# Row statistics moved from VectorE to ScalarE, and a column spread by TensorE instead of two small DMAs, in a four-layer graph network

## The chip, the cores and the metric

The kernel runs on one core of a Trainium2 chip. A core has five engines that run their own instruction streams and meet through semaphores: TensorE (PE, matrix products; the profile lists its weight loads apart as PEld), VectorE (DVE), ScalarE (ACT), GpSimd (POOL), and SyncE (SP), which here only issues DMAs. Products land in PSUM; everything else lives in SBUF. The metric is the device time of one execution in microseconds; lower is better.

## The reference, cut to what matters

There are 128 batches of 128 nodes with 512 features, in float32, and one weighted adjacency matrix of 128x128. Four layers follow each other, each with a residual and a normalisation of every row of 512:

```python
def _layernorm(x):                      # mean and variance over the 512 features of a row
    m, v = mean(x), var(x)
    return (x - m) / sqrt(v + 1e-5)

x = _layernorm(x + (adj @ x) @ W0 + bias0)                       # layer 0
h = x @ W1; s1 = h @ a[:512]; s2 = h @ a[512:]                   # layer 1
e = leaky_relu(s1[:, None] + s2[None, :]) * adj
x = _layernorm(x + elu(softmax(e) @ h + beta * h))
x = _layernorm(x + max over features of relu(adj @ x + b))       # layer 2, per node
q, k, v = split(x @ Wqkv)                                        # layer 3, 8 heads of 64
o = softmax(mask(q @ k.T / 8)) @ v @ Wproj + bproj
x = _layernorm(x + o + _layernorm(o) * gamma + beta3)
```

Layer 1 adds a row logit s1, one number per node, and a column logit s2, which is computed as one number per partition as well but is needed along the free dimension of every partition. Layer 2's term is one number per node. There are five normalisations per batch, 640 in all: one after each layer and one of o.

## The kernel before, in words

A batch is one SBUF tile x of 128 partitions (nodes) by 512 features; 16 such tiles are in flight. `batch(i)` is a Python generator with the chain of steps of one batch through all four layers. Batches are grouped in pairs (G = 2): the pair's queries and keys are computed together (`query_key`, products of 256 columns, L453), and so is layer 1's attention (`attention1`).

The order of the instructions on every engine is fixed at build time by the class `Plan`. Each step asks for an engine with an assumed duration, for buffers, and for a lateness (`yield use("DVE", 0.69, urgent=True)`); `Plan.run` takes again and again the request that can start first, urgent ones and low ranks first among equals, and writes its instructions out in that order. Requests for TensorE are given 1 us after their inputs (MARGIN). So a changed duration or a new step reorders all engines' streams, and on the chip each engine works its stream off strictly in order. The last six batches have ranks lowered by 12, before and after the change alike.

The steps that the change touches:

- `mean_rstd` (L157 to L169): VectorE takes the statistics of a row (`bn_stats`, L161; `bn_aggr`, L163) and adds EPS (L165); GpSimd raises to the power -0.5 (L168). `layernorm_act` then forms -mean*rstd on VectorE (L175) and normalises on ScalarE (L177); `layernorm_dve` normalises on VectorE (L182).
- The operations that write the tile to be normalised: L520 (layer 0: product out of PSUM plus x, VectorE), L545 and L546 (layer 1, VectorE), L561 (layer 2, ScalarE), L647 (o: product plus bias, VectorE), L656 and L659 (layer 3's end, VectorE).
- `attention1` (L376 to L438): the two logits of a pair of batches stand in s, one number per partition; they come from L527, a multiplication with an accumulated sum. The column logits are spread so: VectorE transposes within blocks of 32 (L383), a DMA writes the 256 numbers to memory (L389), a DMA reads them back to every partition (L394, tile z), and VectorE adds the row logit (L400). Leaky relu, adjacency, row maximum, exponential and a transpose through memory (e_d, eT) follow.

Other lines that matter. TensorE: L203 (`mixed`: transposing product into a "tr" bank), L195 (`product`: four accumulating products of 512 columns into an "mm" bank), L554 (layer 2), L583 (scores), L630 (attention times values). PSUM is emptied by ScalarE at L206 (yT), L461 (qkT), L479 (v), L543 (ex), L639 (oT) and by VectorE at L463, L520, L557, L590, L647. Layer 3's probabilities are normalised at L607 and L608, turned at L611 (pt), written by a DMA (p_d) and read back turned (prT) for L630. GpSimd also does three additions per batch (L188). At the start, L342 spreads the columns of W1*a over the partitions with eight TensorE transposes of a broadcast column.

```python
yield use("DVE", 1.0)
nc.vector.bn_stats(st, src); nc.vector.bn_aggr(mv, st)
...
nc.gpsimd.tensor_tensor(rstd, ve, neghalf, op=ALU.pow)
```

Of the kernel before, what the change touches and what calls it, by code (L numbers as in the profile page):

```python
# [8 lines left out]
F32 = mybir.dt.float32  # L9
AF = mybir.ActivationFunctionType  # L10
ALU = mybir.AluOpType
# [4 lines left out]
P = 128  # L16
D = 512
# [4 lines left out]
S = 32  # L22
Q = P // S
ALPHA = 0.2
EPS = 1e-5
# [2 lines left out]

BUFS = {
    "tr": 3, "mm": 3, "sc": 1,  # L30
    "x": 16, "yT": 3, "z": 2, "e": 2, "et": 1, "eT": 2, "ex": 2, "xT": 2, "v": 8, "qkT": 3,
    "pr": 2, "pt": 1, "xt": 2, "prT": 2, "oT": 2, "o": 2,
}
MARGIN = 1.0
# [8 lines left out]
class Plan:  # L43
# [30 lines left out]
    def give(self, slot):  # L74
        name, i = slot
        self.slots[name][i] = self.now
# [38 lines left out]
def gnn_stack_kernel(  # L115
# [28 lines left out]
    use, give, done = plan.use, plan.give, plan.done  # L144

    def buf(shape, name):
        return work.tile(shape, F32, name=name, bufs=BUFS[name])

    def bank(shape, name):
        return ps.tile(shape, F32, name=name, bufs=BUFS[name])  # L150
# [3 lines left out]
        return bass.AP(tensor=src.tensor, offset=src.offset, ap=[[0, P], [1, n]])  # L154


    def mean_rstd(src):  # L157

        yield use("DVE", 1.0)
        st = small.tile([P, 6], F32, name="st")  # L160
        nc.vector.bn_stats(st, src)  # L161
        mv = small.tile([P, 2], F32, name="mv")
        nc.vector.bn_aggr(mv, st)  # L163
        ve = small.tile([P, 1], F32, name="ve")
        nc.vector.tensor_scalar(ve, mv[:, 1:2], EPS, None, op0=ALU.add)  # L165
# [3 lines left out]
        return mv, rstd  # L169

    def layernorm_act(xb):
        mv, rstd = yield from mean_rstd(xb)
        yield use("DVE", 0.21)
        nmr = small.tile([P, 1], F32, name="nmr")
        nc.vector.tensor_scalar(nmr, mv[:, 0:1], rstd, -1.0, op0=ALU.mult, op1=ALU.mult)  # L175
        yield use("ACT", 0.81)
        nc.scalar.activation(xb, xb, AF.Identity, bias=nmr, scale=rstd)  # L177

    def layernorm_dve(xb):
        mv, rstd = yield from mean_rstd(xb)  # L180
        yield use("DVE", 0.67)
        nc.vector.tensor_scalar(xb, xb, mv[:, 0:1], rstd, op0=ALU.subtract, op1=ALU.mult)  # L182

    def pool_add(dst, other, event, after=None):
        if after:
# [24 lines left out]
    def to_rows(turned, scratch):  # L210

        nc.sync.dma_start(scratch, turned)
# [6 lines left out]
    ident = const.tile([P, P], F32, name="ident")  # L219
# [18 lines left out]
    bproj_sb = const.tile([P, D], F32, name="bproj_sb")  # L238
    gamma_sb = const.tile([P, D], F32, name="gamma_sb")
# [136 lines left out]
    def attention1(gr, h):  # L376
        yield gr.logits[h]
        yield scalars_in
        s = gr.s

        yield use("DVE", 0.2)
        st = small.tile([P, 2, Q, S // Q], F32, name="s2")
        nc.vector.transpose(  # L383
            st.rearrange("p i c u -> p i u c"),
            s[:, 2 * h : 2 * h + 2, 1:2, None].to_broadcast([P, 2, S // Q, Q]),
        )
        row = dram.tile([2 * Q, Q, S // Q], F32, name="s_d")
        yield use("SP", 0.1, late=2.0)
        nc.sync.dma_start(  # L389
            row.rearrange("j a u -> a j u"), st[::S].rearrange("p i c u -> p (i c) u")  # L390
        )
        bz = yield use("SP", 0.1, "z", late=2.2)
        z = buf([P, 2, P], "z")
        nc.sync.dma_start(  # L394
            z, row.rearrange("j a u -> (j a u)")[None, :].to_broadcast([P, 2 * P]).rearrange(
                "p (i f) -> p i f", i=2
            ),
        )
        be = yield use("DVE", 2.1, "e", urgent=True)
        nc.vector.tensor_tensor(  # L400
            z, z, s[:, 2 * h : 2 * h + 2, 0:1].to_broadcast([P, 2, P]), op=ALU.add
        )
        e = buf([P, 2, P], "e")
        nc.vector.scalar_tensor_tensor(e, z, ALPHA, z, op0=ALU.mult, op1=ALU.max)
        give(bz)
# [97 lines left out]
    def batch(i):  # L503
        g, b = divmod(i, G)
        h = b // 2
        yield loaded[i]
        gr, xb = group(g), xs[i]
# [3 lines left out]
        yT, by = yield from mixed(xb, adjT)  # L511
# [4 lines left out]
        p = product(lambda k: yT[:, k, :], lambda k: w0_sb[:, k, :])  # L516
        give(by)
        yield biased
        yield use("DVE", 0.69, urgent=True)
        nc.vector.tensor_tensor(xb, p, xb, op=ALU.add)  # L520
        give(bp)
        yield from layernorm_act(xb)
        yield wa_ready
        yield use("DVE", 1.6)
        for j in range(2):
# [3 lines left out]
                accum_out=gr.s[:, b, j : j + 1],  # L529
# [14 lines left out]
        yield use("DVE", 1.5, urgent=True)  # L544
        nc.vector.scalar_tensor_tensor(xb, p, 0.0, xb, op0=ALU.max, op1=ALU.add)  # L545
        nc.vector.scalar_tensor_tensor(xb, ex, 1.0, xb, op0=ALU.min, op1=ALU.add)  # L546
        give(bp)
        give(be)
        yield from layernorm_act(xb)


        bp = yield use("PE", 0.95, "mm", late=0.2, urgent=True)
        p = bank([P, D], "mm")
        nc.tensor.matmul(p, adjT, xb, start=True, stop=True)  # L554
        yield use("DVE", 0.89, urgent=True)
        mx = small.tile([P, 1], F32, name="mx")
        nc.vector.tensor_reduce(mx, p, axis=AX.X, op=ALU.max)  # L557
        nc.vector.tensor_scalar(mx, mx, b2_sb, 0.0, op0=ALU.add, op1=ALU.max)
        give(bp)
        yield use("ACT", 0.81)  # L560
        nc.scalar.activation(xb, xb, AF.Identity, bias=mx)  # L561
        yield from layernorm_dve(xb)


        bt = yield use("DVE", 0.65, "xt")
# [33 lines left out]
        for j in range(H):  # L599
# [3 lines left out]
                accum_out=sums[:, j : j + 1],  # L603
# [41 lines left out]
        bo = yield use("DVE", 0.69, "o", urgent=True)  # L645
# [6 lines left out]
        mv, rstd = yield from mean_rstd(o)  # L652
        yield added
        yield use("DVE", 1.65)
        t1 = one.tile([P, D], F32, name="t1")
        nc.vector.scalar_tensor_tensor(  # L656
            t1, o, mv[:, 0:1], gamma_sb, op0=ALU.subtract, op1=ALU.mult
        )
        nc.vector.scalar_tensor_tensor(xb, t1, rstd, xb, op0=ALU.mult, op1=ALU.add)  # L659
        give(bo)  # L660
        yield from layernorm_dve(xb)
        yield use("SP", 0.1, late=3.0)
        nc.sync.dma_start(out[i], xb)
        give(x_slot[i])
# [37 lines left out]
```

## Time and profile before

| what | value |
|---|---|
| median of 4 runs | 3357.4 us (3354.33 to 3361.61) |
| the profiled execution, its own time | 3357.86 us |
| its span, first to last instruction | 3355.9 us |
| mean granted TensorE clock | 0.996 |
| VectorE busy | 2663.3 us, 79% |
| ScalarE busy | 1186.7 us, 35% |
| GpSimd busy | 934.5 us, 28% |
| mean DMA rate | 91 GB/s |

The statistics on VectorE: L161 takes 348.1 us for 512 tiles x and 87.4 us for 128 tiles o (680 ns each), L163 116.3 us (182 ns each), L165 98.3 us (154 ns each). On ScalarE, an activation over 512 columns takes 722 ns with a per-partition bias (L561), and 813 ns with bias and scale (L177); reading its accumulated sum is an instruction of its own of 189 ns (L601). On VectorE, reading an accumulated sum takes 81 ns (L527).

In the profile an engine's busy time is the union of its instructions' spans. A group is named by line, engine, operation, and tiles as "written<-read". "Idle before" is the engine's idle time ahead of a group, and the arrow names what ended it. The chain that ended last is followed back from the last instruction, at each step to what released it. Lines of the same kind of work carry different numbers before and after the change, since the change adds five lines to the file.

### The profile page before, as it was taken

The numbers are of one execution on the slowest core, as the hardware profiler recorded it, in microseconds if no ns is written. First come the engines' busy times: TensorE is split into PE (matmuls) and PEld (weight loads), VectorE is DVE, ScalarE is ACT, GpSimd is POOL, SyncE is SP. The second block draws the span as 40 slices with busy tenths as digits, with TensorE's granted clock in tenths as the row PEclk, the third lists the DMA queues.
The fourth block names the chain that finished last, engine by engine and source line by source line (L and its number), as shares of the span: only waits on it lengthen the run. The fifth ranks groups of instructions, "written<-read, shape, count | busy, mean of one in ns | idle before, by whom it ended". The sixth has DMA issues, their size and how long they took to land.

```text
span 3355.9 us, 43540 instructions
## 1 busy us (share of the span) xinstructions
PE 3313.4 (99%) x14601; PEld 2056.5 (61%) x14601; DVE 2663.3 (79%) x5527; ACT 1186.7 (35%) x3457; POOL 934.5 (28%) x1031
## 2 busy tenths in 40 slices
PE   9999999999999999999999999999999999999997
PEld 5666656565656566565665666566665665566565
DVE  7877778868877877878788788788788788878875
ACT  2424333333423333333333333333333333343322
POOL 3221322313232232323133223223122234222221
PEclk9999999999999999999999999999999999999998
DMA  4332322332333232232323223323323322322231
GB/s 162 93 112 77 96 91 65 103 95 86 84 95 89 71 96 101 71 108 78 96 85 101 82 79 88 99 77 93 104 81 97 95 79 82 97 78 91 73 108 69
DMA packets 469711, 304.46 MB, mean 91 GB/s; under 512 B 319216, under 2 KB 401264, under 8 KB 469488
## 3 DMA queue, kind: packets, MB, share of 16 engines
q1 hardware_dynamic: 469488, 301.69, 30.1%
q8 instruction: 116, 1.90, 0.2%
q14 instruction: 107, 0.88, 0.1%
HBM read 158.93 MB, written 142.67 MB: 90 GB/s over the span
## 4 chain that ended last, share of the span: by engine, by line
PE 83%; DVE 11%; DMA 4%; issue 1%; ACT 0%; SPq 0%; POOL 0%; POOLq 0%; DVEq 0%; ACTq 0%
PE mm L195 43%; PE mm L453 25%; PE tr L203 5%; PE sc L583 4%; PE tr L630 4%; PE mm L554 3%; DVE st L161 2%; DVE scr L527 2%; DMA z<-s_d 1%; DMA s_d<-s 1%; DVE x L659 1%; DVE x L182 1%; DVE x L520 1%; DVE mv L163 1%; DVE t L656 0%
## 5 line engine op out<-in xcount | busy, mean ns | idle before, releaser
L195 PE MATMUL mm<-w_sb,yT 128*128 128x512 f32 x2048 | 912.3, 594 | 5.5 <-ACT yT L206 4.5
L453 PE MATMUL mm<-xT,wqkv_sb 128*128 128x256 f32 x4096 | 912.6, 381 | 0.7 <-DVE x L520 0.7
L453 PEld LDWEIGHTS mm<-xT,wqkv_sb 128*128 128x128 f32 x4096 | 772.8, 190 | 140.4 <-issue 27.3
L168 POOL TENSOR_TENSOR rstd<-ve,neghalf 128x1 f32<-128x1 f32 x640 | 413.9, 647 | 1290.1 <-DVE ve L165 1098.1
L195 PEld LDWEIGHTS mm<-w_sb,yT 128*128 128x128 f32 x2048 | 381.2, 190 | 454.4 <-issue 434.5
L195 PE MATMUL mm<-wqkv_sb,xT 128*128 128x512 f32 x1024 | 466.3, 598 | 0.0
L601 ACT ACTIVATE pr<-pr,nmx 128x128 f32<-128x128 f32 x1024 | 398.0, 391 | 190.1 <-DVE nmx L597 189.3
L195 PE MATMUL mm<-wproj_sb,oT 128*128 128x512 f32 x1024 | 463.1, 599 | 1.5 <-ACT oT L639 1.5
L188 POOL TENSOR_TENSOR x<-x,o 128x512 f32<-128x512 f32 x128 | 175.7, 1372 | 896.4 <-DVE o L647 797.9
L161 DVE BATCH_NORM_STATS2 st<-x 128x6 f32<-128x512 f32 x512 | 348.1, 680 | 6.7 <-ACT x L561 5.3
L177 ACT ACTIVATE x<-x,nmr,rstd 128x512 f32<-128x512 f32 x256 | 204.7, 810 | 388.0 <-DVE nmr L175 372.9
L195 PEld LDWEIGHTS mm<-wproj_sb,oT 128*128 128x128 f32 x1024 | 191.9, 191 | 224.7 <-issue 218.7
L195 PEld LDWEIGHTS mm<-wqkv_sb,xT 128*128 128x128 f32 x1024 | 189.6, 190 | 201.2 <-issue 192.0
L590 DVE TENSOR_TENSOR pr<-sc,maskb 128x1024 f32<-128x1024 f32 x128 | 156.0, 1219 | 168.5 <-PE sc L583 168.2
L206 ACT COPY yT<-tr 128x512 f32<-128x512 f32 x256 | 147.3, 582 | 202.4 <-PE tr L203 202.2
L527 DVE SCALAR_TENSOR_TENSOR scr<-x,wa_rows 128x512 f32<-128x512 f32 x256 | 200.4, 783 | 23.1 <-ACT x L177 17.0
L188 POOL TENSOR_TENSOR x<-x,beta_sb 128x512 f32<-128x512 f32 x128 | 171.5, 1342 | 161.2 <-DVE xt L567 147.8
L188 POOL TENSOR_TENSOR x<-x,bias_sb 128x512 f32<-128x512 f32 x128 | 181.6, 1429 | 69.7 <-PE tr L203 61.6
L479 ACT COPY v<-mm 128x512 f32<-128x512 f32 x128 | 74.6, 583 | 337.2 <-PE mm L195 337.1
L601 ACT ACTIVATION_READ_ACCUMULATOR pr<-pr,nmx 128x1 f32 x1024 | 193.1, 189 | 0.0
L182 DVE TENSOR_SCALAR x<-x,mv,rstd 128x512 f32<-128x512 f32 x256 | 161.3, 635 | 15.4 <-POOL rstd L168 14.6
L583 PEld LDWEIGHTS sc<-qkT 64*128 64x128 f32 x2048 | 124.8, 187 | 78.0 <-issue 60.1
(62 smaller groups left out, 3483.8 us busy)
## 6 DMA issues: line engine op xcount, KB each, us to landing
p_d<-pt SPq DMA_DIRECT2D x128, 512.0 KB
prT<-p_d SPq DMA_DIRECT2D x128, 512.0 KB
x<-in_x SPq DMA_DIRECT2D x128, 256.0 KB
x_d<-xt SPq DMA_DIRECT2D x128, 256.0 KB
xT<-x_d SPq DMA_DIRECT2D x512, 64.0 KB
out<-x SPq DMA_DIRECT2D x128, 256.0 KB
z<-s_d SPq DMA_DIRECT2D x64, 128.0 KB
e_d<-et SPq DMA_DIRECT2D x64, 128.0 KB
```

What stands on the lines that cost most here:

```text
L161: nc.vector.bn_stats(st, src)
L168: nc.gpsimd.tensor_tensor(rstd, ve, neghalf, op=ALU.pow)
L177: nc.scalar.activation(xb, xb, AF.Identity, bias=nmr, scale=rstd)
L182: nc.vector.tensor_scalar(xb, xb, mv[:, 0:1], rstd, op0=ALU.subtract, op1=ALU.mult)
L188: nc.gpsimd.tensor_tensor(dst, dst, other, op=ALU.add)
L195: nc.tensor.matmul(p, lhs(k), rhs(k), start=(k == 0), stop=(k == K - 1))
L203: nc.tensor.matmul(p[:, k, :], xb[:, k * P : (k + 1) * P], nodes, start=True, stop=True)
L453: nc.tensor.matmul(p[:, j, :], wqkv_sb[:, k, (c + j) * P : (c + j + 1) * P], gr.xT[:, k, :], start=(k == 0), stop=(k == K - 1),)
L527: nc.vector.scalar_tensor_tensor(scr, xb, 1.0, wa_rows[:, j, :], op0=ALU.mult, op1=ALU.mult, accum_out=gr.s[:, b, j : j + 1],)
L583: nc.tensor.matmul(sc[:, j, c, :], gr.qkT[rws, c, nodes], gr.qkT[rws, K + c, nodes], start=True, stop=True,)
L590: nc.vector.tensor_tensor(pr, sc.rearrange("p j c m -> p (j c) m"), maskb[:, None, :].to_broadcast([P, H, P]), op=ALU.add,)
L601: nc.scalar.activation(pr[:, j, :], pr[:, j, :], AF.Exp, bias=nmx[:, j : j + 1], accum_out=sums[:, j : j + 1],)
```

## The change

`mean_rstd` gets the row's sum from its caller: every operation that writes a tile to be normalised now also accumulates the sum over the row (`accum_out`); additions written as `tensor_tensor` become `scalar_tensor_tensor` with a factor of 1.0 for that. VectorE forms nm, the negative mean; ScalarE squares the tile with nm as bias into a tile that nobody reads, and accumulates the sum of squares; VectorE scales and adds EPS; GpSimd's power is as before. The column logits are spread by two TensorE transposes of a broadcast column into a "tr" bank, and VectorE adds the row logit while reading the bank; the DMAs and the block transpose go. The planner's assumed durations are changed with the steps.

```diff
-    def mean_rstd(src):
-
-        yield use("DVE", 1.0)
-        st = small.tile([P, 6], F32, name="st")
-        nc.vector.bn_stats(st, src)
-        mv = small.tile([P, 2], F32, name="mv")
-        nc.vector.bn_aggr(mv, st)
+    def mean_rstd(src, total):
+
+        yield use("DVE", 0.15)
+        nm = small.tile([P, 1], F32, name="nm")
+        nc.vector.tensor_scalar(nm, total, -1.0 / D, None, op0=ALU.mult)
+        yield use("ACT", 1.0)
+        square = one.tile([P, D], F32, name="square")
+        var = small.tile([P, 1], F32, name="var")
+        nc.scalar.activation(square, src, AF.Square, bias=nm, accum_out=var)
+        yield use("DVE", 0.15)
         ve = small.tile([P, 1], F32, name="ve")
-        nc.vector.tensor_scalar(ve, mv[:, 1:2], EPS, None, op0=ALU.add)
+        nc.vector.tensor_scalar(ve, var, 1.0 / D, EPS, op0=ALU.mult, op1=ALU.add)
         yield use("POOL", 0.65, late=0.1, urgent=True)
...
-        nc.vector.tensor_scalar(nmr, mv[:, 0:1], rstd, -1.0, op0=ALU.mult, op1=ALU.mult)
+        nc.vector.tensor_tensor(nmr, nm, rstd, op=ALU.mult)
...
-        nc.vector.tensor_scalar(xb, xb, mv[:, 0:1], rstd, op0=ALU.subtract, op1=ALU.mult)
+        nc.vector.tensor_scalar(xb, xb, nm, rstd, op0=ALU.add, op1=ALU.mult)
...
-        yield use("DVE", 0.2)
-        st = small.tile([P, 2, Q, S // Q], F32, name="s2")
-        nc.vector.transpose(
-            st.rearrange("p i c u -> p i u c"),
-            s[:, 2 * h : 2 * h + 2, 1:2, None].to_broadcast([P, 2, S // Q, Q]),
-        )
-        row = dram.tile([2 * Q, Q, S // Q], F32, name="s_d")
-        yield use("SP", 0.1, late=2.0)
-        nc.sync.dma_start(
-            row.rearrange("j a u -> a j u"), st[::S].rearrange("p i c u -> p (i c) u")
-        )
-        bz = yield use("SP", 0.1, "z", late=2.2)
-        z = buf([P, 2, P], "z")
-        nc.sync.dma_start(
...
+        b0 = yield use("PE", 0.3, "tr", late=0.2, urgent=True)
+        p = bank([P, 2, P], "tr")
+        for i in range(2):
+            nc.tensor.transpose(p[:, i, :], s[:, 2 * h + i, 1:2].to_broadcast([P, P]), ident)
         be = yield use("DVE", 2.1, "e", urgent=True)
-        nc.vector.tensor_tensor(
-            z, z, s[:, 2 * h : 2 * h + 2, 0:1].to_broadcast([P, 2, P]), op=ALU.add
-        )
+        z = one.tile([P, 2, P], F32, name="z")
+        for i in range(2):
+            nc.vector.tensor_scalar(
+                z[:, i, :].rearrange("p (c r) -> p c r", c=Q),
+                p[:, i, :].rearrange("p (r c) -> p c r", c=Q),
+                s[:, 2 * h + i, 0:1], None, op0=ALU.add,
+            )
+        give(b0)
...
-        yield use("DVE", 0.69, urgent=True)
-        nc.vector.tensor_tensor(xb, p, xb, op=ALU.add)
+        yield use("DVE", 0.78, urgent=True)
+        total = small.tile([P, 1], F32, name="total")
+        nc.vector.scalar_tensor_tensor(
+            xb, p, 1.0, xb, op0=ALU.mult, op1=ALU.add, accum_out=total
+        )
...
+        nc.vector.scalar_tensor_tensor(
+            xb, ex, 1.0, xb, op0=ALU.min, op1=ALU.add, accum_out=total
+        )
...
-        yield use("ACT", 0.81)
-        nc.scalar.activation(xb, xb, AF.Identity, bias=mx)
+        yield use("ACT", 0.92)
+        total = small.tile([P, 1], F32, name="total")
+        nc.scalar.activation(xb, xb, AF.Identity, bias=mx, accum_out=total)
...
-        nc.vector.tensor_tensor(o, p, bproj_sb, op=ALU.add)
+        total = small.tile([P, 1], F32, name="total")
+        nc.vector.scalar_tensor_tensor(
+            o, p, 1.0, bproj_sb, op0=ALU.mult, op1=ALU.add, accum_out=total
+        )
...
+        nc.vector.scalar_tensor_tensor(
+            xb, t1, rstd, xb, op0=ALU.mult, op1=ALU.add, accum_out=total
+        )
```

More of the change, by code (lines that the diff above doesn't have):

```diff
@@ L30 @@
     "tr": 3, "mm": 3, "sc": 1,
-    "x": 16, "yT": 3, "z": 2, "e": 2, "et": 1, "eT": 2, "ex": 2, "xT": 2, "v": 8, "qkT": 3,
+    "x": 16, "yT": 3, "e": 2, "et": 1, "eT": 2, "ex": 2, "xT": 2, "v": 8, "qkT": 3,
     "pr": 2, "pt": 1, "xt": 2, "prT": 2, "oT": 2, "o": 2,
@@ L168, in mean_rstd, with layernorm_act, layernorm_dve @@
         nc.gpsimd.tensor_tensor(rstd, ve, neghalf, op=ALU.pow)
-        return mv, rstd
-    def layernorm_act(xb):
-        mv, rstd = yield from mean_rstd(xb)
+        return nm, rstd
+    def layernorm_act(xb, total):
+        nm, rstd = yield from mean_rstd(xb, total)
         yield use("DVE", 0.21)
         nmr = small.tile([P, 1], F32, name="nmr")
-        nc.vector.tensor_scalar(nmr, mv[:, 0:1], rstd, -1.0, op0=ALU.mult, op1=ALU.mult)
+        nc.vector.tensor_tensor(nmr, nm, rstd, op=ALU.mult)
         yield use("ACT", 0.81)
         nc.scalar.activation(xb, xb, AF.Identity, bias=nmr, scale=rstd)
-    def layernorm_dve(xb):
-        mv, rstd = yield from mean_rstd(xb)
+    def layernorm_dve(xb, total):
+        nm, rstd = yield from mean_rstd(xb, total)
         yield use("DVE", 0.67)
-        nc.vector.tensor_scalar(xb, xb, mv[:, 0:1], rstd, op0=ALU.subtract, op1=ALU.mult)
+        nc.vector.tensor_scalar(xb, xb, nm, rstd, op0=ALU.add, op1=ALU.mult)
     def pool_add(dst, other, event, after=None):
@@ L518, in batch @@
         yield biased
-        yield use("DVE", 0.69, urgent=True)
-        nc.vector.tensor_tensor(xb, p, xb, op=ALU.add)
+        yield use("DVE", 0.78, urgent=True)
[3 more added lines that the diff above has]
+        )
         give(bp)
-        yield from layernorm_act(xb)
+        yield from layernorm_act(xb, total)
         yield wa_ready
@@ L543, in batch @@
         nc.scalar.activation(ex, p, AF.Exp)
-        yield use("DVE", 1.5, urgent=True)
+        yield use("DVE", 1.6, urgent=True)
+        total = small.tile([P, 1], F32, name="total")
         nc.vector.scalar_tensor_tensor(xb, p, 0.0, xb, op0=ALU.max, op1=ALU.add)
-        nc.vector.scalar_tensor_tensor(xb, ex, 1.0, xb, op0=ALU.min, op1=ALU.add)
+        nc.vector.scalar_tensor_tensor(
+            xb, ex, 1.0, xb, op0=ALU.min, op1=ALU.add, accum_out=total
+        )
         give(bp)
         give(be)
-        yield from layernorm_act(xb)
+        yield from layernorm_act(xb, total)
         bp = yield use("PE", 0.95, "mm", late=0.2, urgent=True)
@@ L559, in batch @@
         give(bp)
-        yield use("ACT", 0.81)
-        nc.scalar.activation(xb, xb, AF.Identity, bias=mx)
-        yield from layernorm_dve(xb)
+        yield use("ACT", 0.92)
+        total = small.tile([P, 1], F32, name="total")
+        nc.scalar.activation(xb, xb, AF.Identity, bias=mx, accum_out=total)
+        yield from layernorm_dve(xb, total)
         bt = yield use("DVE", 0.65, "xt")
@@ L644, in batch @@
         give(bo)
-        bo = yield use("DVE", 0.69, "o", urgent=True)
+        bo = yield use("DVE", 0.78, "o", urgent=True)
         o = buf([P, D], "o")
-        nc.vector.tensor_tensor(o, p, bproj_sb, op=ALU.add)
+        total = small.tile([P, 1], F32, name="total")
+        nc.vector.scalar_tensor_tensor(
+            o, p, 1.0, bproj_sb, op0=ALU.mult, op1=ALU.add, accum_out=total
+        )
         give(bp)
@@ L651, in batch @@
         plan.start(pool_add(xb, o, added), i)
-        mv, rstd = yield from mean_rstd(o)
+        nm, rstd = yield from mean_rstd(o, total)
         yield added
-        yield use("DVE", 1.65)
+        yield use("DVE", 1.75)
         t1 = one.tile([P, D], F32, name="t1")
         nc.vector.scalar_tensor_tensor(
-            t1, o, mv[:, 0:1], gamma_sb, op0=ALU.subtract, op1=ALU.mult
+            t1, o, nm, gamma_sb, op0=ALU.add, op1=ALU.mult
         )
-        nc.vector.scalar_tensor_tensor(xb, t1, rstd, xb, op0=ALU.mult, op1=ALU.add)
+        total = small.tile([P, 1], F32, name="total")
+        nc.vector.scalar_tensor_tensor(
+            xb, t1, rstd, xb, op0=ALU.mult, op1=ALU.add, accum_out=total
+        )
         give(bo)
-        yield from layernorm_dve(xb)
+        yield from layernorm_dve(xb, total)
         yield use("SP", 0.1, late=3.0)
```

5 lines of the change are left out of this document (removed).

## The prediction

> **What bounds the kernel now.** I read the busy shares and the slices first, then the chain that ended last, then what TensorE waited for, and last the timeline of the end.
>
> ```profile
> span 3355.9 us, 43540 instructions
> ...
> PE 3313.4 (99%) x14601; PEld 2056.5 (61%) x14601; DVE 2663.3 (79%) x5527; ACT 1186.7 (35%) x3457; POOL 934.5 (28%) x1031
> ...
> PE   9999999999999999999999999999999999999997
> ...
> PE 83%; DVE 11%; DMA 4%; issue 1%; ACT 0%; SPq 0%; POOL 0%; POOLq 0%; DVEq 0%; ACTq 0%
> ```
>
> TensorE is busy in 99% of the span, at 90% or more in 39 of 40 slices; the chain is TensorE for 83%. So an instruction added to TensorE lengthens the kernel by about its own time, and work taken from VectorE (79%) pays only where a TensorE gap goes away. All that can be won is span less busy, 3355.9 - 3313.4 = 42.5 us. What ended those gaps:
>
> ```profile
> PE tr L630 <- DMA prT<-p_d: 8.2, 3, 6.2
> PE mm L195 <- ACT yT L206: 4.5, 3, 2.7
> PE mm L554 <- ACT x L177: 3.9, 4, 2.0
> PE sc L583 <- DVE qkT L463: 3.5, 3, 1.4
> PE tr L203 <- DMA x<-in_x: 2.9, 2, 1.9
> PE tr L308 <- DMA adj_sb<-in_adj: 2.8, 1, 2.8
> PE sc L583 <- DVE pr L590: 1.8, 2, 1.2
> PE mm L195 <- ACT oT L639: 1.5, 2, 0.7
> PE mm L554 <- DVE x L520: 1.3, 1, 1.3
> ```
>
> Columns: who waited for what, us in total, times, the longest. The whole list comes to 33.1 us; 9.1 us after the last matmul make up nearly all of the rest. Gaps ended by VectorE add up to 8.2 (3.5 + 1.8 + 1.3 and smaller ones), by ScalarE to 9.9, by DMAs to 15, of which 6.2 is one gap near the end (first the timeline of TensorE, then three lines of the chain in order of time; start, length, what):
>
> ```profile
> 3327.76 3.70 PE L195 MATMUL mm<-wproj_sb,oT 128*128 128x512 f32 x8 [0.74 <-ACT oT L639]
> 3337.68 1.98 PE L630 MATMUL tr<-prT,v 128*64 128x128 f32 x16 [6.21 <-DMA prT<-p_d]
> 3340.38 6.41 PE L195 MATMUL mm<-wproj_sb,oT 128*128 128x512 f32 x8 [0.73 <-ACT oT L639]
> ...
> 3329.93 1.16 DVE pt L611
> 3331.09 0.02 issue
> 3331.11 2.58 DMA p_d<-pt
> ```
>
> After that gap the same work runs slower: 16 matmuls of L630 in 1.98 us (1.09 at other places), 8 of L195 in 6.41 (3.70 above). The granted clock there is 0.50, and 1.00 after an earlier gap of 2.68 us (at 843).
>
> **The change, part by part.**
>
> *1. Column logits by TensorE.* Removed, per pair of batches: one VectorE transpose (L383), two DMAs (L389, L394) and one addition (L400). Added: two TensorE transposes of 128x128 and two VectorE additions out of PSUM. 64 pairs make 128 transposes. The trace has eight of this form (broadcast column, identity), at L342:
>
> ```profile
> 26.96 0.60 PE L342 MATMUL tr<-ident,wa 128*128 128x128 f32 x4
> 27.39 3.60 PE L195 MATMUL mm<-w_sb,yT 128*128 128x512 f32 x8
> ```
>
> Four take 27.39 - 26.96 = 0.43 us from start to start of what follows, 0.109 each, and the neighbours keep their pace. 128 x 0.109 = **+13.9 us**, all on the path. That an instruction alone lasts 272 ns (its group's mean) is pipeline depth; unpipelined it would be 34.8, my upper end. Lower end: if a pair fell into each of the 24 gaps over 0.15 us that the trace has, 24 x 0.22 = 5.3 would be free, leaving 8.6; the gaps are 1% of the span, so I take 13.9.
>
> The Trainium skill, "TensorE: Matmul & The Clock Gate", Part 4, gives about 275 ns for such a transpose inside a kernel. It agrees with the duration of 272 ns, but taken as the price it would make this term 35.2 us and the whole about 3394; the starts 0.109 apart speak against that.
>
> Each pair of transposes is also a new TensorE wait, for VectorE's logits (L527). What queues behind it is the next product. Nearest row: L554, which also waits for a freshly normalised tile, lost 3.9 + 1.3 = 5.2 us over 128 batches; at that rate 64 pairs lose **+2.6** (bounds 0 and 10: four times the rate). The planner gives PE requests 1 us after their inputs, which is why few such waits show.
>
> SP issues 128 DMAs fewer, and the transfers queued behind them (x_d, p_d, xT) leave earlier. SP had waited 91 us at L389 and 51.7 at L394. Only 3.0 us of mid-kernel TensorE gaps end on a DMA, so 0 is taken, -3 the bound. VectorE had waited 67.2 us for z; it now waits for TensorE instead.
>
> *2. Variance on ScalarE.* VectorE loses 640 of each of L161, L163 and L165: 348.1 + 87.4 + 116.3 + 98.3 = 650.1 us. It gains 1280 one-column operations (nm, ve) at L165's 154 ns, 197.1, and 512 accumulator reads at 81 ns (from L527's), 41.5. Part 1 there: -17.7 (L383) - 32.3 (L400) + 128 x 0.291 (a 128x128 out of PSUM, L310) = -12.8. VectorE becomes 2663.3 - 650.1 + 197.1 + 41.5 - 12.8 = 2239 us, 67%. ScalarE gains 640 squarings, each like L561 (722 ns) and an accumulator read (189 ns, L601's); the reads overlap partly, so 640 x 0.72 to 0.91 = 461 to 583, plus at most 24 for L561's sums: 1660 to 1794 us, 49 to 53%. Neither nears TensorE.
>
> The cost is in the order, not the sum. A norm was VectorE, GpSimd, VectorE; it is now VectorE, ScalarE, VectorE, GpSimd, VectorE. On ScalarE, evictions that TensorE needs (yT, oT, v, qkT, ex) stand behind squarings of 0.9 us. On VectorE, ve waits for the squaring, and behind it stand evictions of L463, L520, L590 and L647. For the gaps I scale by busy time: those ended by ScalarE (9.9) by 1730/1187, +4.5; those by VectorE (8.2) by 2239/2663, -1.3; **+3** in all. Bounds: the VectorE ones all gone, -8.2; three in a hundred of ScalarE's 640 evictions late by a squaring, 640 x 0.03 x 0.91 = +17.5.
>
> *3. The end.* In the changed program's order the last pt (L611) stands behind only o, nm, rs, pr and ve; before, two further evictions and statistics stood between. From o's start at 3322.6: 0.77 + 0.1 + 0.2 + 1.23 + 0.15 + 1.2 ends at 3326.3, against 3331.1. prT lands 6.5 later (2.58 + 3.81 + 0.1), at 3332.9 rather than 3337.5. But the last oT but one is queued on ScalarE behind the squaring of the second o, which VectorE can release only at about 3328.9; oT ends at 3330.5 (3327.7 before), so its product ends at 3334.1, L630 at 3335.2, the last product at 3339.5 (3346.8 before) if the clock stays full. The chain after it grows from 9.1 to 10.1: two norms of nm + squaring + ve and two hops (about 1.45) in place of 1.05, and two accumulator reads. So -6.3 at best. The new gap, 3327.0 to 3330.5, is 3.5 us long, between the 2.68 that kept the clock and the 6.21 that halved it; halved, the three pieces lose up to 6.5 and nothing is won. I take **-4**, nearer the best end since 3.5 is nearer 2.68; bounds -6.3 and +1.
>
> The same page's Part 1 says that the clock halves after a whole idle window of about 3.4 us, in windows that run freely. By it, 3.5 us seldom spans a whole window, and the term would be -6; the rows alone leave that open.
>
> *4. The start.* The first transposes stand about 37.9 us in, behind wa_rows (copied by 33.4) and four passes of L527 (0.73 each, one of them up to 1.7): 36.3 to 37.3. Just in time: 0, bounds -2.4 (the three gaps before 75 us gone: 1.4 + 0.7 + 0.2) and +3.
>
> **Sum.** 13.9 + 2.6 + 3 - 4 + 0 = +15.5 us. The profiled execution took 3357.86 (span 3355.9 and 2.0 around it) and would take 3373.4; it lies 0.46 above the median of four, 3357.4. Predicted: **3373**, 0.46% slower. Runs of before spread over 7 us, so about 0.2%, 6.7 us, is what a measurement can tell from no change: "same" is 3350.7 to 3364.1.
>
> **Rivals.**
>
> *VectorE's relief pays for the transposes (ends at "same").* Place: the TensorE gaps ended by VectorE, and the end. For it: VectorE is the only other engine above half, and most of ScalarE's idle time was spent waiting for it. Against it: its gaps are small and spread. Price, with no new waits: 13.9 - 8.2 - 6.3 = -0.6, 3357. It decides once more than 13.9 - 6.7 = 7.2 us is won back. To be faster by over 0.2%, 20.6 of the 42.5 idle microseconds have to go; 9 of them are the last chain and 5.7 the first loads, which nothing here touches.
>
> *ScalarE's queue becomes the brake.* 13.9 + 17.5 + 2.6 - 4 = +30, 3387. For it: 640 pieces of 0.9 us in a strict queue in front of evictions. Against: at 53% it has room, and the planner books 1.0 us for each squaring, more than the rows give.
>
> *Transposes at full duration.* 34.8 in place of 13.9: 3394. Against: the starts at L342.
>
> That the edit does not do what it says I exclude: the changed program has 128 more TensorE instructions, 128 DMAs fewer, 640 squarings and still one table load.
>
> **How the numbers follow.** Forecast (3364 to 3381) 0.53; ScalarE's queue 0.19; full-length transposes 0.05; VectorE's relief, "same", 0.17; more than that won, faster, 0.06. Slower is 0.53 + 0.19 + 0.05 = 0.77. The range, 3357 to 3392, runs from the relief rival's value to just past the queue rival's; outside lie faster, a part of "same" and the transposes' case. The forecast's own is 3364 to 3381.
>
> **What would show it.** TensorE busy about 3327 us with 14729 instructions, transposes 0.11 apart; VectorE near 67%, ScalarE near 50%; a prT gap at the end under 3 us; waits of TensorE for ScalarE (yT, oT, x) up by some microseconds. I am wrong if TensorE's busy time hardly rises, if its gaps fall under 30 us or rise past 60, or if the new transposes show long waits for the logits.

## The result: 0.2% faster, where 0.5% slower was forecast

The changed kernel takes 3350.4 us (median of 29 runs, 3348.8 to 3352.7), the kernel before 3357.0 (47 runs): ratio 0.9979, 95% interval 0.9974 to 0.9984. The forecast was 3373, with a range from 3357; 3350.4 lies just past the bound of "same" (3350.7), in the outcome that was given a chance of 0.06. The page of the changed kernel, with the lines that answer to those of before:

```profile
span 3350.9 us, 45044 instructions
...
PE 3320.9 (99%) x14729; PEld 2065.6 (62%) x14729; DVE 2281.6 (68%) x5399; ACT 1676.9 (50%) x4865; POOL 915.6 (27%) x1031
...
PE 92%; DVE 4%; DMA 1%; ACT 1%; issue 1%; POOL 0%; SPq 0%; POOLq 0%; DVEq 0%; ACTq 0%
```

The loads are as worked out: 128 TensorE instructions more, VectorE at 2282 us (2239 forecast), ScalarE at 1677 (1660 to 1794). TensorE's busy time rose by 7.5 us only, and its gaps shrank. What it waited for:

```profile
PE mm L198 <- ACT oT L638: 6.0, 3, 4.4
PE tr L386 <- DVE scr L522: 5.0, 5, 1.8
PE tr L206 <- DMA x<-in_x: 3.1, 2, 1.8
PE tr L311 <- DMA adj_sb<-in_adj: 2.7, 1, 2.7
PE tr L206 <- DMA eT<-e_d: 1.3, 2, 0.9
PE tr L629 <- DMA prT<-p_d: 1.1, 2, 0.6
PE mm L552 <- DVE x L541: 0.2, 1, 0.2
PE mm L552 <- ACT x L180: 0.2, 1, 0.2
```

The whole list is 19.6 us, against 33.1 before. Of VectorE's waits little but the new ones remains (L386 for the logits, 5.0); of ScalarE's, in spite of 490 us more work there, little but one gap at the end.

**How the time is split below.** The idle list shows only part of what TensorE loses. A 512-column matmul lasts 594 ns but the next can start 429 ns after it, so a wait of up to 165 ns shows as busy time. The Trainium skill, "Trainium Kernel Development and Optimization", under "Performance Expectations", says that matmul busy time is a bad metric for how close a kernel is to roofline, because matmuls are pipelined. This case agrees: the stretch called middle below shows 18.4 us of gaps in the kernel before and takes 68.1 us more than the spacing of its matmuls. So I add up the shortest spacing of every matmul from the trace's start times (429 ns at 512 columns, 216 at 256, 112 at L203, 109 for a transpose of a column, 68 and 64 on average at L583 and L630) and call it *work*. *Start* is the time until 60 us of work are issued, less these; *end* the time from the last 150 us of work to the end of the span, less these; *middle* what remains. Part of the middle is no wait at all but the regular cost of changing from one kind of matmul to another; the lowest middle in any kernel here is 41 us (with the transposes doubled). Each split is taken from one profiled execution, and executions of one kernel lie up to 10 us apart (before, 3353 to 3363), so differences of 2 or 3 us between two rows mean nothing.

| kernel | median us | ratio to before, 95% | work | start | middle | end |
|---|---|---|---|---|---|---|
| before | 3357.0 | | 3252.4 | 11.2 | 68.1 | 24.2 |
| changed | 3350.4 | 0.9974 to 0.9984 | 3266.4 | 10.8 | 52.6 | 21.2 |

The parts add up to the spans. So the change cost 14.0 us of work, won 15.5 in the middle, 3.0 at the end and 0.4 at the start. Of the 15.5, 10.2 are visible gaps (18.4 to 8.2). Another 3.4 are the clock: twice in the middle of the kernel before, the granted clock was 0.50 for 3.41 us (from 1379.8 and from 2212.7), which loses half of that each time, and never in the middle of the changed kernel. Two pieces of TensorE's timeline before:

```profile
1378.58 0.72 PE L583 MATMUL sc<-qkT 64*128 64x128 f32 x8 [1.41 <-DVE qkT L463]
...
1380.60 4.90 PE L195 MATMUL mm<-wqkv_sb,xT 128*128 128x512 f32 x8
```

```profile
2212.24 3.41 PE L554 MATMUL mm<-x,adjT 128*128 128x512 f32 x4 [2.03 <-ACT x L177]
```

The 8 matmuls at 1380.60 take 3.60 at full clock, and those at half clock start 854 ns apart in place of 429. The experiments ask where the 15.5 come from, and how much of it all belongs to the change.

### The profile page after: what moved, and what is told of

It reads as the page before. It is cut to its first block, busy times and chain, and to the rows that moved or that the text cites. A ratio compares the mean times of both kernels' runs of the same rounds, so it can differ in the third digit from the quotient of the medians.

```text
span 3350.9 us, 45044 instructions
## 1 busy us (share of the span) xinstructions
PE 3320.9 (99%) x14729; PEld 2065.6 (62%) x14729; DVE 2281.6 (68%) x5399; ACT 1676.9 (50%) x4865; POOL 915.6 (27%) x1031
## 4 chain that ended last, share of the span: by engine, by line
PE 92%; DVE 4%; DMA 1%; ACT 1%; issue 1%; POOL 0%; SPq 0%; POOLq 0%; DVEq 0%; ACTq 0%
PE mm L198 49%; PE mm L445 26%; PE tr L206 6%; PE sc L582 4%; PE tr L629 4%; PE mm L552 3%; DVE scr L522 1%; PE tr L386 0%; DVE x L542 0%; DVE x L185 0%; POOL rstd L171 0%; ACT x L180 0%; DVE xt L566 0%; DVE x L662 0%; DVE x L541 0%
## 5 line engine op out<-in xcount | busy, mean ns | idle before, releaser
L171 POOL TENSOR_TENSOR rstd<-ve,neghalf 128x1 f32<-128x1 f32 x640 | 395.9, 627 | 1321.5 <-DVE ve L168 1108.0
L165 ACT ACTIVATE square<-x,nm 128x512 f32<-128x512 f32 x512 | 367.7, 718 | 181.7 <-DVE nm L161 158.6
L522 DVE SCALAR_TENSOR_TENSOR scr<-x,wa_rows 128x512 f32<-128x512 f32 x256 | 213.0, 832 | 39.7 <-ACT x L180 34.3
L185 DVE TENSOR_SCALAR x<-x,nm,rstd 128x512 f32<-128x512 f32 x256 | 161.0, 631 | 74.0 <-POOL rstd L171 72.4
L165 ACT ACTIVATE square<-o,nm 128x512 f32<-128x512 f32 x128 | 92.2, 720 | 232.3 <-DVE nm L161 217.0
```

Source lines behind the costliest of these rows:

```text
L165: nc.scalar.activation(square, src, AF.Square, bias=nm, accum_out=var)
L185: nc.vector.tensor_scalar(xb, xb, nm, rstd, op0=ALU.add, op1=ALU.mult)
L522: nc.vector.scalar_tensor_tensor(scr, xb, 1.0, wa_rows[:, j, :], op0=ALU.mult, op1=ALU.mult, accum_out=gr.s[:, b, j : j + 1],)
```

## Experiments

### Each part by itself

The variance pass alone is the changed kernel with the logits' steps of before; the transposes alone are the kernel before with the new `attention1`. Both have been run in two orders: the second differs by one assumed duration of the planner, which changes no instruction, only the order in which they are written.

```diff
-        yield use("POOL", 1.35)
+        yield use("POOL", 1.31)
```

> The changed kernel with its column logits spread by two DMAs as before: the variance pass alone. Theory A (taking the statistics from VectorE frees TensorE of waits; the transposes cost their 13.9 us on top): TensorE busy 3301 to 3309 us, gaps as small as in the changed kernel, so 13 to 22 us below it, about 3328 to 3338, ratio to before about 0.992. Theory B (the gain comes from the DMAs and the VectorE wait for z that went): at or above before, 3355 to 3368. Theory C (any new order of the streams moves the time by some 10 us): anywhere from 3340 to 3365.

> The kernel before with the column logits spread by TensorE: part 1 alone, statistics still on VectorE. Theory A: before plus 13.9 for the transposes and 3 to 8 for their waits on a VectorE at 79%, 3370 to 3380, ratio 1.004 to 1.007. Theory B: below before, about 3340 to 3350. Theory C: 3355 to 3385.

> The variance pass alone, as in the first experiment, with GpSimd's addition planned at 1.31 us: a second order of it, and a candidate for the fastest. If the gain of 13 us in the middle belongs to the variance pass and not to one order: middle loss 51 to 57 again, total 3332 to 3342, faster than before by at least 0.4%. If it was the order's: middle loss 60 to 70.

> The transposes alone, a second order. If VectorE's waits for z had cost TensorE about 6 us, as the first order says: middle loss 57 to 63, total 3350 to 3362 by its end. If that was the order's: 65 to 70, and 3360 or more.

| kernel | median us | ratio to before, 95% | work | start | middle | end |
|---|---|---|---|---|---|---|
| variance alone | 3340.7 | 0.9936 to 0.9961 | 3252.4 | 13.7 | 52.4 | 19.9 |
| variance alone, second order | 3335.9 | 0.9918 to 0.9943 | 3252.4 | 13.4 | 49.0 | 20.0 |
| transposes alone | 3353.5 | 0.9978 to 0.9996 | 3266.4 | 13.0 | 50.6 | 22.8 |
| transposes alone, second order | 3352.4 | 0.9973 to 0.9990 | 3266.4 | 13.2 | 47.7 | 24.1 |

(In the texts on record up to the second orders the middle leaves out the last 60 us alone, which puts some of the end into it. By that cut the variance pass alone stands at 54 and 50.4, the transposes alone at 60 and 50.0: their first order waits 3.25 us for prT at 3257, between the two cuts. So the second order of the transposes came out below its 57 to 63.) Theory A missed on the transposes: they pay for themselves although VectorE's statistics stay. Theory B missed on the variance pass, which is the faster part, and 3340.7 is also just outside A's 3328 to 3338; 3353.5 lies in the range of no theory. Against the 68.1 of before, either part alone takes 16 to 20 us from the middle, and both together no more than one. They are two cures for the same loss, or two losses that cover each other.

### The price of a transpose

```diff
-        b0 = yield use("PE", 0.3, "tr", late=0.2, urgent=True)
+        b0 = yield use("PE", 0.52, "tr", late=0.2, urgent=True)
         p = bank([P, 2, P], "tr")
-        for i in range(2):
+        for i in (0, 1, 0, 1):
             nc.tensor.transpose(p[:, i, :], s[:, 2 * h + i, 1:2].to_broadcast([P, P]), ident)
```

> The changed kernel with every transpose of the logits done twice into the same bank: 128 more of them. If they cost the 0.109 us between their starts, 13.9 us above the changed kernel, 3364, with TensorE busy up by 14. At their full duration of 272 ns it would be 35 us, 3385. If gaps hide them, under 8 us.

3372.5 us, 22 above the changed kernel, but not by the transposes alone: its end costs 39.6 against 21.2, and its middle 41 against 52.6, so without the end it is only 2 us longer. The total does not tell the price. TensorE's busy time does better:

```profile
PE 3333.3 (99%) x14857; PEld 2081.7 (62%) x14857; DVE 2261.7 (67%) x5399; ACT 1674.2 (50%) x4865; POOL 906.6 (27%) x1031
```

3333.3 - 3320.9 = 12.4 us for 128 more, 0.097 each. The start times tell it directly: what follows the four starts 0.437 us after the first of them (median of the 64 groups), and 0.218 after the first of a pair in the changed kernel, 0.109 for each. An instruction of their group lasts 280 ns in the mean, and that is not what it costs:

```profile
L386 PE MATMUL tr<-ident,s 128*128 128x128 f32 x128 | 26.2, 280 | 5.0 <-DVE scr L522 5.0
```

### How much is the order?

Nothing but the assumed duration of GpSimd's addition is changed, from 1.35 to 1.33 or 1.37 us, in the kernel before and in the changed one.

> The kernel before with one assumed duration of the planner changed (GpSimd's addition 1.33 us in place of 1.35): the same instructions, another order. Theory C (the order that the planner happens to write decides over some 10 us, and the kernel before has a costly one, above all at its end, where pt is written late and the clock drops): 3342 to 3352, TensorE busy 3304 to 3309. Theory D (the gain of the changed kernel lies in its parts, and orders differ little): 3354 to 3361, as before.

> The same with 1.37 us. Theory C: not the time of the 1.33 one, but like it below before, 3342 to 3355. Theory D: 3354 to 3361.

> The changed kernel with GpSimd's addition planned at 1.33 us. Theory C: off the changed kernel's 3350.4 by several microseconds either way, 3340 to 3362; and over both pairs the changed kernel's mean above that of before by up to the 13.9 us of the transposes. Theory D: 3347 to 3354.

> The changed kernel with 1.37 us. Theory C: 3340 to 3362, another time than with 1.33. Theory D: 3347 to 3354.

| kernel | median us | ratio to before, 95% | work | start | middle | end |
|---|---|---|---|---|---|---|
| before, 1.33 | 3345.7 | 0.9951 to 0.9976 | 3252.4 | 12.8 | 62.9 | 16.7 |
| before, 1.37 | 3345.2 | 0.9955 to 0.9980 | 3252.4 | 11.7 | 64.3 | 14.4 |
| changed, 1.33 | 3368.2 | 1.0021 to 1.0046 | 3266.4 | 11.3 | 47.9 | 40.5 |
| changed, 1.37 | 3379.4 | 1.0057 to 1.0085 | 3266.4 | 10.5 | 52.6 | 48.1 |

Theory C holds, and more strongly than expected (3368 and 3379 lie above its 3340 to 3362): the same instructions in another order move the time by 12 us in the kernel before and by 29 in the changed one. In each pair of new orders the changed kernel is the slower, by 23 and 34 us; the orders that were compared first happen to be the slowest of the three for before and the fastest of the three for the change. The middle depends on it less in these two kernels: 62.9 to 68.1 before, 47.9 to 52.6 after, without overlap (before with 1.35 and with 1.33 share much of their order, so these two count for less than two). The end does. The timeline of TensorE near the end of the changed kernel with 1.37:

```profile
3314.25 16.93 PE L445 MATMUL mm<-xT,wqkv_sb 128*128 128x256 f32 x64 [14.88 <-DMA xT<-x_d]
...
3353.11 1.98 PE L629 MATMUL tr<-prT,v 128*64 128x128 f32 x16 [12.69 <-DMA prT<-p_d]
3355.76 6.30 PE L198 MATMUL mm<-wproj_sb,oT 128*128 128x512 f32 x8 [0.68 <-ACT oT L638]
```

The last pair of batches comes late, and with no other batch left TensorE idles twice, for 14.9 us until xT has gone through memory and for 12.7 until prT has. Is it the end alone? The last six batches were given another rank in the slow order with 1.33; TensorE's stream stays the same for 985 of 1144 rows:

```diff
-            plan.start(batch(i), i if i < NB - 6 else i - 12)
+            plan.start(batch(i), i if i < NB - 6 else i - 16)
```

(and the same 12 to 16 at the two places in `group`).

> The changed kernel in the order with 1.33 us (3368.2 us), with the last six batches' ranks lowered by 16 in place of 12; the order of TensorE's stream stays the same up to row 985 of 1144. If the slow orders of the changed kernel are slow by their last 150 us alone: start and middle as there (11.3 and 47.9 to within 4), the end 18 to 26 cheaper, 3342 to 3350. If by the middle too: above 3355.

3343.0 us, ratio 0.9948 to 0.9973: start 10.6, middle 48.9, end 15.7. The 25 us went from the end and nowhere else. Its last matmuls:

```profile
3303.80 7.13 PE L198 MATMUL mm<-wqkv_sb,xT 128*128 128x512 f32 x16
3310.86 1.97 PE L629 MATMUL tr<-prT,v 128*64 128x128 f32 x32
3312.76 7.13 PE L198 MATMUL mm<-wproj_sb,oT 128*128 128x512 f32 x16
```

So the slow orders of the changed kernel were slow by their last batches, and the change can be had at 3343 as well as at 3379.

### What the transposes take away

VectorE waits for z, in order, and evictions that TensorE needs stand behind. In the kernel before, on VectorE and then on TensorE:

```profile
2964.59 0.43 DVE L400 TENSOR_TENSOR z<-z,s 128x256 f32<-128x256 f32 x1 [5.61 <-DMA z<-s_d]
...
2966.30 1.22 DVE L590 TENSOR_TENSOR pr<-sc,maskb 128x1024 f32<-128x1024 f32 x1
```

```profile
2967.57 1.16 PE L583 MATMUL sc<-qkT 64*128 64x128 f32 x16 [1.17 <-DVE pr L590]
```

5.61 us of waiting for z, then the four operations from z to the row maximum of e (L400 to L411), then the eviction of the scores, for which TensorE idles 1.17 us. The idle list names pr L590; the z that held it up is one step further back. The test keeps the DMAs and only tells the planner that z comes later, so that VectorE gets other work first:

```diff
-        bz = yield use("SP", 0.1, "z", late=2.2)
+        bz = yield use("SP", 0.1, "z", late=4.2)
```

with 1.37 us for GpSimd's addition, in the kernel before (k1) and with the variance pass alone (k3).

> The kernel before with two assumed durations of the planner changed: GpSimd's addition 1.37 us, and the arrival of z 4.2 us after its DMA is issued in place of 2.2, so that VectorE is given other work before it. No part of the change. Loss in the middle from here on leaves out the last 150 us of TensorE's work: 64.3 us in the kernel with 1.37 alone, 50.6 and 47.7 with the transposes in place of the DMAs. If VectorE's waits for z with evictions queued behind them are what the transposes take away: those waits fall from 58 to under 20 us, middle loss 46 to 56, total 3328 to 3340. If not: 60 to 68 and 3340 to 3352.

> The variance pass alone with the late z and 1.37 us: the work of the kernel before on TensorE, both causes of middle loss taken away without a transpose. If both are real: waits for z under 20 us, middle loss 42 to 50, 3324 to 3334, the fastest of all; faster than before by 0.7 to 1.0%. If the late z does nothing: middle loss 49 to 53, 3333 to 3341.

| kernel | median us | ratio to before, 95% | work | start | middle | end |
|---|---|---|---|---|---|---|
| before, late z | 3336.8 | 0.9928 to 0.9953 | 3252.4 | 11.4 | 53.4 | 15.0 |
| variance alone, late z | 3324.2 | 0.9892 to 0.9919 | 3252.4 | 10.6 | 43.6 | 15.5 |

VectorE's waits for z, of the kernel before and of the two:

```profile
DVE z L400 <- DMA z<-s_d: 67.2, 41, 5.6
```

```profile
DVE z L400 <- DMA z<-s_d: 9.3, 6, 4.6
```

```profile
DVE z L403 <- DMA z<-s_d: 17.5, 16, 2.9
```

The waits go from 67.2 (58.3 in the order with 1.37) to 9.3, and the middle from 64.3 to 53.4, at a VectorE that is as busy as before (2652 us). That is most of the 14 to 17 us that the transposes alone take from the middle, so waiting for z is the likeliest name of the loss that they remove; it rests on one order of k1 and one of k3, and other pairs below differ by as much between two orders. The traces bear it out in part. In the order with 1.37, 6.8 of the 17.2 us of TensorE's gaps in the middle fall within 8 us after a wait for z of over 0.3 us, in k1 0.2 of 8.0; in the kernel before it is 7.1 of 18.0 (18.4 with the smallest), so most of its visible gaps are not behind such a wait. One number in the planner did it as well, without 14 us of TensorE. The variance pass with the late z is the fastest kernel here, 3324.2 us, 0.95% below before:

```profile
span 3322.1 us, 44988 instructions
...
PE 3301.2 (99%) x14601; PEld 2053.3 (62%) x14601; DVE 2274.9 (68%) x5399; ACT 1676.2 (50%) x4865; POOL 907.5 (27%) x1031
```

### What the variance pass takes away

Alone it leaves the waits for z as they were (72.2 and 72.0 us in its two orders) and still lowers the middle by 13 to 16, against the mean of 65.1 in three orders of before. What it takes away is mostly other gaps: those of TensorE in the middle that do not come within 8 us after such a wait for z are 10.9, 9.7 and 10.4 us in three orders of before, but 3.3 and 2.7 with the variance pass alone, while those behind a wait for z go from 7.1, 5.8 and 6.8 to 5.6 and 3.3. That is nearness in time, not a chain that was followed. Three ideas on the cause were tried.

Idea one: VectorE's load. 640 spare passes over a constant tile fill it again, off all chains.

```diff
+    def spare():
+        yield use("DVE", 0.69)
+        st = small.tile([P, 6], F32, name="st")
+        nc.vector.bn_stats(st, w0_sb[:, 0, :])
...
+        plan.start(spare(), 1000)
         yield use("DVE", 0.15)
```

> The changed kernel with 640 extra statistics passes of 0.68 us on VectorE, over a constant tile, with no reader and on no chain: VectorE's load goes back to about 81%, everything else stays. Theory A, if it is VectorE's load that makes TensorE wait: the gaps come back, 12 to 22 us above the changed kernel, 3362 to 3372. If it is the length of the chain of a norm and not the load: within 4 us of the changed kernel.

3344.1 us (0.9947 to 0.9972), with VectorE at 2598 us and a middle of 44.2: lower than without the passes, and below both ranges of the text. With the transposes in place, and in this one order, load is not it.

Idea two: a block of a microsecond on the chain of a norm. The spare pass is put into the step that forms nm, in two orders (the second with 1.39 for GpSimd's addition); and the other way round the kernel before asks for its three statistics operations one by one.

```diff
-        yield use("DVE", 0.15)
+        yield use("DVE", 0.84)
+        st = small.tile([P, 6], F32, name="st")
+        nc.vector.bn_stats(st, w0_sb[:, 0, :])
         nm = small.tile([P, 1], F32, name="nm")
```

> The changed kernel with a statistics pass of 0.69 us over a constant tile put on VectorE inside the step that forms nm, so that it lies on every norm's chain and in one block with it; its result has no reader. Middle loss means TensorE's time between its first and its last 60 us of work, less that work at the shortest spacing of each kind of matmul: 70.3, 65.6 and 66.1 us in three orders of the kernel before, 54.2, 55.6 and 53.3 in three of the changed one. Theory E (VectorE's block of a microsecond on the chain of a norm is what delays the evictions that TensorE waits for): middle loss back at 62 to 70, about 3358 to 3368 if the end stays cheap. Theory F (it is not VectorE's work at all, on the chain or off it): middle loss 43 to 57, 3340 to 3352 with a cheap end.

> A second order (GpSimd's addition planned at 1.39 us) of the changed kernel with a spare statistics pass on every norm's chain. Theory E: middle loss 57 to 66 again (60.4 in the first, 47.9 to 52.6 without the pass). If the first was the order's: 46 to 54.

```diff
-        yield use("DVE", 1.0)
+        yield use("DVE", 0.65)
         st = small.tile([P, 6], F32, name="st")
         nc.vector.bn_stats(st, src)
+        yield use("DVE", 0.2)
         mv = small.tile([P, 2], F32, name="mv")
         nc.vector.bn_aggr(mv, st)
+        yield use("DVE", 0.15)
```

> The kernel before with the three operations of its statistics requested from the planner one by one (0.65, 0.2, 0.15 us) in place of one block of 1.0: the same work, and urgent evictions may be put between. Theory E: middle loss 53 to 62 in place of 66 to 70, about 3333 to 3345 with a cheap end. Theory F: 64 to 71, 3342 to 3357.

The first order of the block on the chain gave 3362.2 us and a middle of 60.4 (69.9 by the cut of its text), as theory E wants; the second gave 3347.1 and 42.0, below even the 46 to 54 of its text. The block alone does not bring the loss back, so theory E falls as it was put; why the first order lost more stays open. Splitting gave 3346.0, a middle of 57.1 (67.1 by the cut of its text, where E wanted 53 to 62): some 6 us under the other orders of before, or nothing, by where one cuts.

Idea three: room on VectorE, which lets it catch up after a wait for z. Then the variance pass with the DMAs of before, filled again, should lose as much as before. The spare passes of idea one, in the variance pass alone, in two orders (1.35 and 1.31):

> The variance pass alone, the logits by DMA with z's waits as in the kernel before, and 640 spare statistics passes of 0.69 us over a constant tile on VectorE, off all chains. Theory G (the variance pass gives VectorE room, so that its waits for z no longer reach TensorE; either cure does the work of both): with VectorE full again and the waits for z still there, the middle loss is back at 58 to 68. Theory H (something else in the variance pass): 44 to 54, as without the spare passes (52.4, 49.0).

> A second order of the same, GpSimd's addition planned at 1.31 us. Theory G: 58 to 68. Theory H: 44 to 54. One of each leaves it open.

| kernel | median us | ratio to before, 95% | work | start | middle | end |
|---|---|---|---|---|---|---|
| variance alone, filled | 3331.2 | 0.9899 to 0.9933 | 3252.4 | 12.5 | 49.0 | 15.6 |
| variance alone, filled, second order | 3347.7 | 0.9957 to 0.9981 | 3252.4 | 12.3 | 62.1 | 21.5 |

One of each. The lower one waits for z 41.6 us in all, the higher one 64.0, which fits, but two orders do not settle it; and with the variance pass alone 5.6 and 3.3 us of gaps still come behind waits for z, so "no longer" in theory G is too strong. What can be said: every kernel whose middle is above 57 has either long waits for z on a VectorE at 78% or more, or is the first order with the block on the chain. Each of these kernels also has the granted clock at 0.50 for 3.4 or 6.8 us in its middle, and no other kernel has. That the variance pass lowers the middle is shown in two orders of it; by what, stays open.

## Why the prediction was wrong

*What held.* 13.9 us for the transposes: their spacing is 0.109 in pairs and in fours, and doubling them added 12.4 of busy time. (The 275 ns that are quoted there are stated for bf16 tiles; these are float32.) The new waits for the logits: 2.6 forecast, 5.0 visible, inside the bounds of 0 to 10. The end: -4 forecast, -3.0 measured, and the order as drawn up. prT no longer makes TensorE wait there, because pt stands ahead, and oT behind the squaring of the second o makes a new gap:

```profile
3323.43 1.09 PE L629 MATMUL tr<-prT,v 128*64 128x128 f32 x16
3328.94 6.39 PE L198 MATMUL mm<-wproj_sb,oT 128*128 128x512 f32 x8 [4.42 <-ACT oT L638]
3335.26 1.09 PE L629 MATMUL tr<-prT,v 128*64 128x128 f32 x16
```

It was forecast at 3.5 us and is 4.42, and the clock fell: 8 matmuls take 6.39 us, and the granted clock is 0.54 from 3328 to 3335. The -4 rested on a clock that mostly holds; halved, "nothing is won". It halved, but for one of the three pieces only (L629 after it takes 1.09 us again, where before both L630 and L195 were slow), so the nearness of -3.0 is partly luck. Nor do the prediction's two rows, 2.68 us that kept the clock and 6.21 that halved it, bound the gap that does it. The same trace halves it after gaps of 1.41 and 2.03 us, and in the order with 1.33 it is 0.51 from 846.8 to 850.2, by another gap of 2.68 us. The Trainium skill, "TensorE: Matmul & The Clock Gate", Part 1, has the clock halved after a whole idle window of about 3.4 us; 4.42 and 6.21 us agree with that, 1.41 and 2.03 do not. The length of the gap alone does not decide here, and what does was not tested. The start: 0 forecast, -0.4. ScalarE's queue, a rival at 0.19, cost nothing to speak of: at 1677 us its gaps in TensorE's list outside the end are under 2 us. Two small slips in the working change nothing: 1186.7 + 461 makes 1648 for ScalarE, not 1660, and the whole list of gaps has 25, not 24.

*What failed: the middle.* Two steps of the sum, "0 is taken, -3 the bound" for the removal of the DMAs and z's waits, and "**+3** in all" for the gaps under the variance pass. Together they stood for +3 (bounds -11 and +17.5), with the 2.6 of new waits for +5.6; the middle measured -15.5 with those waits in it. Two errors are behind both. First, the visible gaps were taken for the whole loss: gaps in the middle fell from 18.4 to 8.2 us, and another 5.3 us were never visible as gaps, 3.4 of them the two stretches at half clock. Second, gaps were put down to the engine that ended them and scaled by its busy time. Those ended by ScalarE were to grow by 4.5; in the middle they fell from 7.0 us to 1.1, with 490 us more work on ScalarE. Those ended by VectorE were to fall by 1.3; the old ones went from 8.2 to 0.2. The 67.2 us that VectorE waited for z were read off the list and priced at nothing, since no TensorE gap named a z; late z alone was worth 11 us of middle in the one order tried. Who ended a gap is not who made it late.

*What was not seen at all.* But for the start and the end, the prediction treated a new order as the old with terms added, and nowhere the order of before as one of several. The planner rewrites all five streams after any change, and the end of its order decides: 14 to 48 us. Without the end, work, start and middle come to 3331.7, 3328.1 and 3328.4 in the three orders of before and to 3329.8, 3325.6, 3329.5 and 3325.9 in the four of the changed kernel (the last shares its middle with the second): the change as such pays 14 us of TensorE and wins about as much in these orders; these runs cannot tell which is more. Its measured gain of 0.2% is smaller than what either kernel gains or loses by changing an assumed 1.35 us into 1.37. The rival "VectorE's relief pays for the transposes", given 0.17 at 3357, came nearest, and VectorE's old gaps went as it says. But TensorE's middle won about twice its -8.2, ScalarE's gaps went too, and that it was VectorE's relief is not shown: the transposes alone pay for themselves with VectorE at 79%.

## What to carry to other kernels

Where a planner or scheduler writes the order, time two or three neutral variations of it for both versions before crediting a change with less than 1%, and look at the last batches apart from the rest. An engine that works strictly in order and waits for a small transfer can hold up whatever is queued behind: follow a gap on the bound engine one step further back than its releaser, and first try telling the scheduler a later arrival, which costs no engine anything. When an engine shows 99% busy, count the spacing of its instructions, and look at its granted clock, not at its idle time alone.

## What the runs showed of the hardware that was not expected

A transpose of a broadcast column between other products costs its 109 ns of spacing, in pairs (0.218 us) and in fours (0.437), although it lasts 273 to 280 ns. A gap of 4.42 us on TensorE is paid again: the eight matmuls after it took 6.39 us against 3.70. Much shorter gaps can be, too: after 1.41 and 2.03 us in the kernel before, the granted clock was 0.50 for 3.41 us, while one of 2.68 us kept it at 1.00. And 490 us of squarings on ScalarE, in front of evictions in a strict order, left TensorE's waits for it in the middle lower than before, 1.1 us against 7.0.
